# Signs of the last convolution worked out in an early stage, and a partial sum kept on chip

## The chip, the cores and the metric

The kernel runs on one core of one Trainium2 chip. The metric is the device time of one execution in microseconds (us), lower is better. Two versions are compared by a ratio: the mean time of one kernel's fast runs over the mean of the other's fast runs in the same rounds, on the same chip. It is therefore not quite the ratio of the medians that are also quoted. A program counts as faster or slower from 2%. Every kernel was also run once under the profiler, and all times inside an execution are from those single profiles.

## The reference

Two layers on an input of 2 images, 256 channels, 128 x 128 points. Layer 0 is a group norm, three deformable depthwise branches (dilations 1, 9, 12), their sum with a 1x1 convolution, a layer norm, an MLP and a second layer norm. Layer 1 is a group norm and a 3x3 convolution whose weights are reduced to three values.

```python
def _branch(x, w_off, w_def, lw, lb, pad, dil):
    off = _conv(x, w_off, pad, dil)                  # 18 offsets per point
    y = _deform_dw(x, off, w_def, pad, dil)          # bilinear samples, 9 taps per channel
    return gelu(_ln2d(y, lw, lb))
x1, x2, x3 = (_branch(...) for dilation in (1, 9, 12))
out = _ln2d(x1 + x2 + x3 + conv1x1(x), n1_w, n1_b)
out = _ln2d(mlp(out) + out, n2_w, n2_b)              # layer 0: x = x + out of gn(x)
# layer 1
tern = where(w/max > 0.05, 1, where(w/max < -0.05, -1, 0))    # the signs
wq = where(tern > 0, Wp * tern, where(tern < 0, Wn * tern, tern))
x = x + conv3x3(gn(x), wq) + bias
```

## The kernel before

The program has three stages. The *offset stage* computes group-norm statistics of an image, then walks over it in 32 groups of four rows ("columns" below): it normalises, convolves on TensorE, and stores tables of samples and weights ("hats") in memory. Image 1 follows image 0. The *sampling stage* multiplies hats and table rows on TensorE, ScalarE empties PSUM into `ev`, and VectorE adds into three rings of rows, one per branch. A *tail* with its own small scheduler takes finished rows out of the rings through norms and MLP, step by step between the samples; after the last sample it runs alone, which I call the *drain*. The *last stage* is the 3x3 convolution with signs.

The statistics loop of the offset stage uses one tag with three buffers, `xt`:

```python
for b in range(NB):
    for c in range(KC):
        for g0 in range(0, NGRP, XT):
            xt = ap.tile([P, XT * NG], F32, name="xt", tag="xt", bufs=3)   # 1 MB
            nc.sync.dma_start(xt, x[b, ...])
            for j in range(XT):
                nc.vector.bn_stats(stats[:, c, g0 + j, :], xt[:, j * NG : (j + 1) * NG])
    mean, rstd = group_norm(stats, f"gn1_{b}", gps)
    ...
    phase_a(b, ap, psum, k)          # the 32 columns of this image
```

The program's text is put into the engines' order by a scheduler, so an instruction may run well before the place where it is written. The tail of one group of rows of one branch, cut:

```python
if br == 0:
    nc.sync.dma_start(gv, v); return           # written out
other = self.tile("other")
nc.sync.dma_start(other, gv)                   # read again
if br == 1:
    v = v + other                              # VectorE
    nc.sync.dma_start(gv, v); return           # the sum of two is written out
...                                            # br == 2: S = v + 1x1 convolution
pin(nc.vector.tensor_tensor(S, S, other, ALU.add))
```

The rings hold 12, 28 and 32 rows, the tail has 9 buffers of 512 KB (`RINGS = (12, 28, 32)`, `VBUFS = 9`). An addition of two rows is split in two where a ring wraps. The last stage first calls `quantise`: it loads the 2.36 MB of weights, finds their largest absolute value, works out exact thresholds, and makes signs (two comparisons and a difference for each of 18 slices) and sums of signs, all on VectorE, before the convolution can begin.

Of the kernel before, what the change touches and what calls it, by code (L numbers as in the profile page):

```python
# [9 lines left out]
F32 = mybir.dt.float32  # L10
I32 = mybir.dt.int32
U32 = mybir.dt.uint32
BF16 = mybir.dt.bfloat16
# [6 lines left out]
P = 128  # L20
W = 128
# [28 lines left out]
RINGS = (12, 28, 32)  # L50
BRS = (0, 1, 2)
NORMS = 3
VBUFS = 9
# [14 lines left out]
def conv_preact_kernel(ctx: ExitStack, tc: tile.TileContext, t: dict, out: bass.AP):  # L68
# [19 lines left out]

    def load(name, shape, src):
        tl = const.tile(shape, F32, name=name)  # L90
        nc.sync.dma_start(tl, src)
        return tl

    gmask = load("gmask", [P, P], t["gmask"])
    convs = [
# [18 lines left out]

    def dram(name, shape):
        return [scratch.tile(shape, F32, name=f"{name}{b}", tag=f"{name}{b}") for b in range(NB)]
# [8 lines left out]
    yd = scratch.tile([3, C, HW], F32, name="yd")  # L125

# [33 lines left out]
    def phase_a(b, pool, psum, k):  # L160
# [160 lines left out]
        for g in range(NGRP):  # L321
            columns(g)
            while G < H // ZG and min(H - 1, G * ZG + ZG - 1 + max(DILS)) < (g + 1) * R:
                parts = offsets(G)
                for j in range(ZG // R):
                    make_hats(G * (ZG // R) + j, parts, j * R)
                G += 1

    with ExitStack() as actx:
# [18 lines left out]
        nc.sync.dma_start(k["wz"], t["wz"].rearrange("(k p) n -> p k n", p=P))  # L348
        nc.sync.dma_start(k["shift"], t["shift"])
        hatw = ap.tile([P, 2, NTAP * NH], F32, name="hatw32")  # L350
        nc.sync.dma_start(hatw, t["hatw"])
        nc.vector.tensor_copy(k["hatw"], hatw)
        pattern = ap.tile([P, NG], F32, name="pattern")
        nc.sync.dma_start(pattern[HALF : HALF + NPAT], t["pattern"])
        for pl in k["planes"]:
            nc.vector.tensor_copy(
                pl[HALF : HALF + NPAT, 1, :], pattern[HALF : HALF + NPAT]
            )
        for parts in k["parts"]:
            nc.vector.memset(parts, 0.0)  # L360
        XT = min(4, NGRP)
        for b in range(NB):
            stats = ap.tile([P, KC, NGRP, 6], F32, name=f"stats1_{b}", tag=f"stats1_{b}")
            for c in range(KC):
                for g0 in range(0, NGRP, XT):
# [7 lines left out]
                    for j in range(XT):  # L373
                        nc.vector.bn_stats(stats[:, c, g0 + j, :], xt[:, j * NG : (j + 1) * NG])
            mean, rstd = group_norm(stats, f"gn1_{b}", gps)
# [7 lines left out]
            phase_a(b, ap, psum, k)  # L383
# [8 lines left out]
    beyond = nc.values_load(flag[0:1, 0:1], min_val=0, max_val=1)  # L392

# [4 lines left out]
    class Tail:  # L398
# [4 lines left out]
        def __init__(self, pool, psum, pin):  # L403
            self.pool, self.psum, self.pin = pool, psum, pin
            self.waiting, self.running = deque(), []
            self.now = self.last = self.norms = 0
            self.read = set()
# [4 lines left out]
        def may(self, item):  # L412

            others = sum(r[2] for r in self.running if r is not item)
            if self.running and item is not self.running[0]:
                young = others - self.running[0][2] + item[3]
                return young <= VBUFS - PEAK and others + item[3] <= VBUFS
            return others + item[3] <= VBUFS

# [85 lines left out]
        def branch(self, b, br, g, y):  # L505
# [18 lines left out]
            yield 1, 1 + br  # L524
            other = self.tile("other")
            nc.sync.dma_start(other, gv)
            if br == 1:
                yield 2
                pin(nc.vector.tensor_tensor(v, v, other, ALU.add))
                yield 2  # L530
                nc.sync.dma_start(gv, v)
                return
# [12 lines left out]
        def finish(self, b, g, S, other, xn):  # L545
# [3 lines left out]
            for m in range(KC):  # L549
# [8 lines left out]
                )  # L558
            pin(nc.vector.tensor_tensor(S, S, other, ALU.add))
# [65 lines left out]
    def sample_near(pool, psum, k):  # L625

        pin = tc.keep_in_program_order
        tail = Tail(pool, psum, pin)
# [294 lines left out]
    def quantise(pool, signs=None):  # L923

        wq = pool.tile([P, KC, 9, C], F32, name="wq", tag="wq", bufs=1)
        nc.sync.dma_start(wq, t["l1w"].rearrange("(k p) t o -> p k t o", p=P))
        scale = []
        for name in ("wp", "wn"):
            s = pool.tile([P, 1], F32, name=name, tag=name, bufs=1)
            nc.sync.dma_start(s, t[name].partition_broadcast(P))  # L930
            scale.append(s)
        wp, wn = scale
        nc.vector.tensor_scalar(wn, wn, -1.0, None, ALU.mult)

        def col(name):
            return pool.tile([P, 1], F32, name=name, tag=name, bufs=1)

        own, m, mh, ml, pr, er, z, nc_ = (
            col(f"q_{i}") for i in ("own", "m", "mh", "ml", "pr", "er", "z", "nc")
        )  # L940
        nc.vector.tensor_reduce(
            own, wq.rearrange("p k t o -> p (k t o)"), AX.X, ALU.max, apply_absolute_value=True
        )
        nc.gpsimd.partition_all_reduce(m, own, P, bass.bass_isa.ReduceOp.max)  # L944



        def ts(dst, a, s1, op0, s2=None, op1=None):
            nc.vector.tensor_scalar(dst, a, s1, s2, op0, *(() if op1 is None else (op1,)))

        ts(mh, m, 4097.0, ALU.mult)
        nc.vector.tensor_tensor(ml, mh, m, ALU.subtract)
        nc.vector.tensor_tensor(mh, mh, ml, ALU.subtract)
        nc.vector.tensor_tensor(ml, m, mh, ALU.subtract)
        ts(pr, m, THR, ALU.mult)
        nc.vector.scalar_tensor_tensor(er, mh, THR_HI, pr, ALU.mult, ALU.subtract)
        nc.vector.scalar_tensor_tensor(er, mh, THR_LO, er, ALU.mult, ALU.add)
        nc.vector.scalar_tensor_tensor(er, ml, THR_HI, er, ALU.mult, ALU.add)
        nc.vector.scalar_tensor_tensor(er, ml, THR_LO, er, ALU.mult, ALU.add)
        nc.vector.scalar_tensor_tensor(er, m, THR_HALF_ULP, er, ALU.mult, ALU.add)  # L960

        ts(z, m, 0.0, ALU.is_equal)
        nc.vector.tensor_tensor(pr, pr, z, ALU.add)
        ts(nc_, er, -1.0, ALU.mult)
        for k in range(KC):
            for tap in range(9):
                w = wq[:, k, tap, :]
                up = pool.tile([P, C], F32, name="up", tag="up", bufs=1)
                ts(up, w, pr, ALU.subtract, er, ALU.is_ge)
                dn = pool.tile([P, C], F32, name="dn", tag="dn", bufs=1)  # L970
                ts(dn, w, pr, ALU.add, nc_, ALU.is_le)
                if signs is not None:
                    nc.vector.tensor_tensor(signs[:, k, tap, :], up, dn, ALU.subtract)  # L973
                    continue
                ts(up, up, wp, ALU.mult)
                nc.vector.scalar_tensor_tensor(w, dn, wn, up, ALU.mult, ALU.add)
        return wq

# [51 lines left out]
    def phase_c_signs(b, pool, psum, cring, signs, sums, wp, half):  # L1030
# [9 lines left out]
        JC = RC // 2  # L1040
        for g in range(H // RC):
# [4 lines left out]
            for k in range(KC):  # L1046
                nc.sync.dma_start(xl[:, k, rows, :], xv[:, k, lo:hi, :])
            xc = cring[g % len(cring)]
            for k in range(KC):
# [16 lines left out]
                left = D.rearrange("p i j w -> p (i j) w")  # L1066
                for i in range(2):
                    part = xc[:, i, k, :, 1 : 1 + W]
                    nc.scalar.copy(part, left)  # L1069
                    nc.vector.tensor_tensor(  # L1070
                        left if i == 0 else xc[:, 2, k, :, 1 : 1 + W], left, part, ALU.subtract
                    )
            for m in range(KC):
                pc = psum.tile([P, 4, 512], F32, name="pc", tag="pc", bufs=2)

                for bank, t in ((0, 0), (1, 3), (2, 1), (3, 2)):
# [3 lines left out]
                    for j, (k, kx, i) in enumerate(todo):  # L1080
                        w = (
                            signs[:, k, (t // 3 * 2) * 3 + kx] if t % 3 == 0
                            else sums[:, k, t - 1, kx]
# [30 lines left out]

    wpn = small.tile([P, 2], F32, name="wpn", tag="wpn", bufs=1)
    for i, name in enumerate(("wp", "wn")):
        nc.sync.dma_start(wpn[:, i : i + 1], t[name].partition_broadcast(P))
    eq = const.tile([P, 1], I32, name="eq")
    nc.vector.tensor_tensor(eq, wpn[:, 0:1], wpn[:, 1:2], ALU.is_equal)
    same = nc.values_load(eq[0:1, 0:1], min_val=0, max_val=1)  # L1120

    with tc.If(same > 0) as cmp:  # L1122
        with ExitStack() as cctx:
# [10 lines left out]
            signs = cp.tile([P, KC, 9, C], BF16, name="signs")  # L1134
            quantise(cp, signs)

            sums = cp.tile([P, KC, 2, 3, C], BF16, name="sums")
            for k in range(KC):
                nc.vector.tensor_tensor(
                    sums[:, k, 0], signs[:, k, 0:3], signs[:, k, 6:9], ALU.add  # L1140
                )
                nc.vector.tensor_tensor(
                    sums[:, k, 1], sums[:, k, 0], signs[:, k, 3:6], ALU.subtract
                )
                nc.vector.tensor_tensor(
                    sums[:, k, 0], sums[:, k, 0], signs[:, k, 3:6], ALU.add
                )
# [109 lines left out]
```

## Time and profile before

| | before |
|---|---|
| median of the given runs | 7754.24 us (7741.94 to 7755.99) |
| span in the profile | 7751.0 us |
| start of the first sampling matmul | 960.3 us |
| first to last sampling matmul | 5556.9 us |
| drain (to the end of the tail's last addition on VectorE) | 139.4 us |
| from there to the 95th matmul of the last convolution | 84.5 us |
| the rest | 1009.9 us |

The five pieces add up to the span. They are read from the start and end of named instructions in the trace. The page's first part, each engine's busy time with its share of the span and its instructions, and two of its costliest groups (line, engine, operation, tiles, count | busy us, mean ns | idle time before, and what ended it):

```profile
PE 7065.1 (91%) x37984; PEld 5377.1 (69%) x37984; DVE 6136.4 (79%) x12892; ACT 4818.2 (62%) x10138; POOL 708.7 (9%) x1292
...
L762 PE MATMUL pm<-A,xs 128*128 128x180 f32 (+2 forms) x22288 | 3609.6, 318 | 466.8 <-ACT ev L771 438.3
...
L740 DVE SCALAR_TENSOR_TENSOR ring<-ev,defw,ring 128x256 f32<-128x256 f32 (+3 forms) x6272 | 2774.5, 462 | 359.7 <-ACT ev L771 175.2
```

TensorE (PE) is the fullest engine over the whole, and the sampling matmuls wait almost only for ScalarE's eviction (438.3 of 466.8 us of idle time). The last row is the ring addition that shorter rings split more often. The transfers that the change removes are these (same page, list of DMA issues: KB each, us from issue to landing):

```profile
g12d<-T SPq DMA_DIRECT2D x128, 512.0 KB, 7.5
other<-g12d SPq DMA_DIRECT2D x128, 512.0 KB, 10.3
```

Half of each, 64 writes and 64 reads, belong to the sum of two branches.

### The profile page before, as it was taken

How to read it: one execution, taken by the hardware profiler on the slowest of the kernel's cores; microseconds unless marked ns; L12 is line 12 of the kernel's file. 1: busy time of each engine (PE TensorE's matmuls, PEld its weight loads, DVE VectorE, ACT ScalarE, POOL GpSimd, SP SyncE). 2: the span in 40 equal slices, each digit the busy share in tenths (PEclk: the TensorE clock that was granted, in tenths of full speed). 3: DMA queues.
4: the chain of work that ended last, by engine and by line, in shares of the span. 5: the costliest groups of instructions: out<-in, count | busy, mean ns of one | idle time of the engine just before them, and what ended most of it. 6: DMA issues, size and time to landing. Idle time of an engine off the chain costs nothing. (4 is left out here: it accounts for less than half of the span.)

```text
span 7751.0 us, 115301 instructions
## 1 busy us (share of the span) xinstructions
PE 7065.1 (91%) x37984; PEld 5377.1 (69%) x37984; DVE 6136.4 (79%) x12892; ACT 4818.2 (62%) x10138; POOL 708.7 (9%) x1292
## 2 busy tenths in 40 slices
PE   5999888999999999999988999999999998699999
PEld 3555587787877788777777778777887776244444
DVE  6666568888888888888678888888888885677676
ACT  1344366777777777777766777777777776333232
POOL 0000000111111111111101111111111111000000
PEclk9999889999999999999999999999999998799999
DMA  8776799999999999998699999999999994212121
GB/s 296 212 197 190 191 235 249 249 255 251 246 252 252 252 247 251 254 245 229 184 235 247 255 249 250 247 251 255 247 249 253 251 241 133 85 74 75 70 75 49
DMA packets 1011325, 1652.64 MB, mean 213 GB/s; under 512 B 120800, under 2 KB 573200, under 8 KB 1006360
## 3 DMA queue, kind: packets, MB, share of 16 engines
q1 hardware_dynamic: 993304, 1611.57, 77.7%
q10 hardware_dynamic: 17408, 33.56, 1.4%
q8 instruction: 304, 4.98, 0.3%
q14 instruction: 309, 2.53, 0.1%
HBM read 1376.69 MB, written 268.09 MB: 212 GB/s over the span
## 5 line engine op out<-in xcount | busy, mean ns | idle before, releaser
L762 PE MATMUL pm<-A,xs 128*128 128x180 f32 (+2 forms) x22288 | 3609.6, 318 | 466.8 <-ACT ev L771 438.3
L762 PEld LDWEIGHTS pm<-A,xs 128*128 128x128 f32 x22288 | 3407.1, 195 | 680.7 <-ACT ev L771 545.8
L740 DVE SCALAR_TENSOR_TENSOR ring<-ev,defw,ring 128x256 f32<-128x256 f32 (+3 forms) x6272 | 2774.5, 462 | 359.7 <-ACT ev L771 175.2
L771 ACT COPY ev<-pm 128x360 f32<-128x360 f32 (+2 forms) x5572 | 2235.8, 455 | 1131.6 <-DVE ring L740 462.9
L689 DVE TENSOR_TENSOR A<-hy,hx 128x768 f32<-128x768 f32 x1130 | 1022.3, 946 | 424.2 <-DMA hx<-hats 246.5
L487 ACT ACTIVATE T<-T,rs 128x256 f32<-128x256 f32 x1280 | 662.5, 593 | 3.3 <-POOL rs L483 3.2
L480 POOL TENSOR_SCALAR rs<-mv 128x4 f32<-128x4 f32 x320 | 120.7, 377 | 4981.0 <-DVE mv L478 2392.1
L1085 PE MATMUL pc<-cring,signs 128*128 128x512 bf16 x2304 | 521.9, 385 | 57.8 <-DVE signs L973 24.3
L1085 PE MATMUL pc<-cring,sums 128*128 128x512 bf16 x2304 | 510.3, 380 | 0.0
L446 PE MATMUL hp<-T,w 128*128 128x512 f32 x1024 | 492.7, 606 | 12.9 <-ACT T L565 12.9
L476 DVE BATCH_NORM_STATS2 st<-T 128x6 f32<-128x256 f32 x1280 | 446.8, 411 | 23.6 <-ACT T L468 23.6
L1085 PEld LDWEIGHTS <-signs 128*128 128x128 bf16 x2304 | 227.3, 99 | 341.8 <-issue 46.6
L203 PE MATMUL pz<-wz,xa 128*128 128x486 f32 x1024 | 456.7, 579 | 4.3 <-DVE zr L210 4.3
L446 PE MATMUL h<-hT,w 128*128 128x512 f32 x1024 | 460.1, 592 | 0.0
L1085 PEld LDWEIGHTS <-sums 128*128 128x128 bf16 x2304 | 225.4, 98 | 274.4
L515 ACT ACTIVATE T<-zc,bb,bw 128x512 f32<-128x512 f32 x384 | 278.7, 781 | 220.2 <-PE zc L499 219.7
L733 ACT ACTIVATE ring<-ev,defw 128x256 f32<-128x256 f32 (+1 forms) x788 | 392.2, 503 | 24.1
L499 PEld LDWEIGHTS zc<-ident,T 128*128 128x128 f32 x2560 | 325.9, 151 | 97.5 <-issue 61.5
L1093 ACT ACTIVATE o<-xl,l1b 128x1024 f32<-128x1024 f32 x64 | 73.5, 1149 | 505.7 <-DMA out_x<-o 408.3
L499 PE MATMUL zc<-ident,T 128*128 128x128 f32 x2560 | 368.7, 289 | 20.1 <-ACT T L487 13.9
L1069 ACT CAST cring<-D 128x2048 bf16<-128x2048 f32 x128 | 243.3, 1902 | 225.0 <-PE pc L1085 153.7
L482 POOL TENSOR_TENSOR rs<-rs,mhalf 128x4 f32<-128x4 f32 x320 | 368.3, 1151 | 0.0
(120 smaller groups left out, 5814.0 us busy)
## 6 DMA issues: line engine op xcount, KB each, us to landing
hy<-hats SPq DMA_DIRECT2D x1114, 384.0 KB, 6.5
hx<-hats SPq DMA_DIRECT2D x1114, 384.0 KB, 7.4
xs<-table SPq DMA_DIRECT2D x1876, 128.0 KB, 4.4
g12d<-T SPq DMA_DIRECT2D x128, 512.0 KB, 7.5
other<-g12d SPq DMA_DIRECT2D x128, 512.0 KB, 10.3
hats<-hb SPq DMA_DIRECT2D x192, 240.0 KB, 4.3
hats<-hb SPq DMA_DIRECT2D x192, 192.0 KB, 3.4
xl<-x1d SPq DMA_DIRECT2D x56, 640.0 KB, 3.9
```

What stands on the lines that cost most here:

```text
L203: nc.tensor.matmul(pz[:, 0:NZ], lhsT=xt[:, c, r, :], rhs=k["wz"][:, c, :], start=c == 0, stop=c == KC - 1,)
L446: nc.tensor.matmul(out, lhsT=w, rhs=v, start=i == 0, stop=i == n - 1)
L476: pin(nc.vector.bn_stats(st[:, j, :], Tv[:, j, :]))
L482: nc.gpsimd.tensor_tensor(rs[:, 0, :], rs[:, 0, :], mhalf[:, 0:NB4], ALU.pow)
L487: nc.scalar.activation(Tv[:, j, :], Tv[:, j, :], AF.Identity, scale=rs[:, 0, j : j + 1], bias=rs[:, 1, j : j + 1],)
L499: nc.tensor.transpose(zc[:, j * P : (j + 1) * P], Tv[:, j, c * P : (c + 1) * P], ident)
L689: nc.vector.tensor_tensor(dst, hy[:, i0:i1].rearrange("p i t w -> p t i w"), hx[:, i0:i1].rearrange("p i t w -> p t i w"), ALU.mult,)
L733: pin(nc.scalar.mul(dst, src, w))
L740: pin(nc.vector.scalar_tensor_tensor(dst, src, w, dst, ALU.mult, ALU.add))
L762: nc.tensor.matmul(pm[:, j, 0:n], lhsT=xts[b, Rt][T + j][:, c * P : (c + 1) * P], rhs=A[:, m0:m1, AO + (T + j) * CI : AO + (T + j + 1) * C ...
L771: nc.scalar.copy(ev[:, m0:m1, T * CI : (T + 2) * CI].rearrange("p m (t j) -> p t m j", j=CI), pm[:, :, 0:n].rearrange("p t (m j) -> p t m ...
L1085: nc.tensor.matmul(pc[:, bank, :], lhsT=w[:, m * P : (m + 1) * P], rhs=xc[:, i, k, t * JC : (t + 1) * JC, kx : kx + W], start=j == 0, stop ...
```

## The change

It has four intents: take the work for the signs out of the gap before the last convolution and put it where VectorE has room; load constants behind the first image's statistics instead of ahead of them; keep the sum of the first two branches in a buffer till the third branch adds to it; and pay for two more tail buffers with four rows less in two of the rings. The core of the diff, cut:

```diff
-RINGS = (12, 28, 32)
+RINGS = (8, 24, 32)
-VBUFS = 9
+VBUFS = 11
 ...                          # constants: load() only collects, load_now() issues
+    def store_signs(pool):   # a generator, one step per yield
+        def chunk(k, i):
+            w = pool.tile([P, 5, C], F32, name="wk", tag="xt", bufs=3)...
+            nc.sync.dma_start(w, t["l1w"]...[:, k, taps])
+        ...                  # 4 chunks: maxima; thresholds
+        for k in range(KC):
+            sg = pool.tile([P, 15, C], BF16, name="sg", tag="xt", bufs=3)
+            ...              # 2 chunks each: signs and sums of signs
+            nc.sync.dma_start(signd[:, k], sg)
+            yield
 ...
         for g in range(NGRP):
             columns(g)
+            next(beside, None)           # a step of store_signs beside each column
 ...
+        beside = store_signs(ap)
         for b in range(NB):
             ...                          # statistics, xt ring
+            if b == 0:
+                load_now()               # constants, hats' weights, patterns
             ...
-            phase_a(b, ap, psum, k)
+            phase_a(b, ap, psum, k, beside)
 ...
+            kept = self.keep and br == 2
+            yield 1, 2 if kept else 1 + br
+            if kept:
+                while (b, g) not in self.kept:
+                    yield 1
+                other = None
             ...
             if br == 1:
                 pin(nc.vector.tensor_tensor(v, v, other, ALU.add))
+                if self.keep:
+                    self.kept[b, g] = v
+                    return
 ...                          # last stage: one load of ready signs behind the first
+            if first:        # two activation loads; the first tile's split in quarters
+                nc.sync.dma_start(signs, signd)
+                for i in ORDER:
+                    for k in range(KC):
+                        split(xc, k, Ds[k], i, i + 1)
-            quantise(cp, signs)
```

The chunks and the signs take turns in the three `xt` buffers with the statistics' tiles.

## The prediction

> **What bounds the kernel now.** I first read the timeline of the page (its slices), to find the stages, then a table of stretches cut at the stage borders, then the chain of waits, then the instructions in order of time at each border. The kernel has three stages: offsets and tables (0 to 938 us, one start per image), sampling with a tail of normalisations and MLP (944 to 6657), and the last convolution (6660 to 7745). The stretches (TensorE, its weight loads, VectorE, ScalarE, GpSimd, granted clock, DMA share, GB/s):
>
> ```profile
> 0.00:80.00 80.00, 2.52 (x11) 2.23 (x12) 48.35 (x87) 1.28 (x1) 1.40 (x7) 1.00 0.84 305
> 80.00:944.00 864.00, 833.09 (x3391) 464.42 (x3389) 567.89 (x1259) 345.32 (x640) 2.03 (x2) 0.98 0.74 209
> 1100.00:3780.00 2680.00, 2464.70 (x14286) 2119.70 (x14287) 2279.69 (x5118) 1978.87 (x4432) 340.31 (x616) 0.98 0.94 246
> 6500.00:6660.00 160.00, 133.73 (x478) 78.09 (x476) 62.59 (x166) 84.91 (x162) 25.11 (x56) 0.83 0.20 66
> 6660.00:6740.00 80.00, 29.37 (x94) 11.05 (x95) 70.72 (x140) 18.66 (x11) 1.07 (x2) 0.62 0.25 94
> ```
>
> Offsets: TensorE 96% busy, VectorE 66%, DMA 74%: TensorE binds, VectorE and DMA have room. Sampling: TensorE 92%, VectorE 85%, DMA 94% at once; TensorE is the floor and idles 8%. The border at 6660: TensorE works 29 of 80 us while VectorE is full. Why TensorE idles in sampling, from the chain of waits between 1100 and 6500 (total us, times, longest):
>
> ```profile
> PE pm L762 <- ACT ev L771: 418.1, 266, 7.9
> ACT ev L771 <- DVE ring L740: 440.4, 242, 8.7
> DVE A L689 <- DMA hx<-hats: 202.4, 140, 7.3
> DVE A L689 <- DMA other<-g12d: 23.1, 9, 2.6
> ```
>
> TensorE waits for ScalarE to empty PSUM, ScalarE for VectorE to finish with the evicted tile, and VectorE, some of the time, for a transfer. I followed this through a period of six units (two row tiles, three branches, about 86 us, 64 periods in all), with the instructions of the trace between the middle rows of both images: TensorE idles 5.9 us of a period, 2.7 in the first unit and 2.2 in the fifth. In the first VectorE is full (18.9 of 18.8 us, overlaps counted) plus 1.5 us waiting for hats; in the fifth it is full with 0.3 us of such waits. In the second unit VectorE waits 1.0 us for DMA, but TensorE has no gap there.
>
> The border to the last stage, in order of time:
>
> ```profile
> 6659.76 0.38 SPq L926 DMA_DIRECT2D wq<-in_l1w  x1
> 6668.26 4.95 DVE L941 TENSOR_REDUCE q_own<-wq 128x1 f32<-128x4608 f32 x1 [1.81 <-DMA wq<-in_l1w]
> 6673.19 0.87 DVE L154 TENSOR_SCALAR xn<-xl,gn2s_mean,gn2s_rstd 128x1152 f32<-128x1152 f32 x1
> 6713.16 10.48 PE L1085 MATMUL pc<-cring,signs 128*128 128x512 bf16 x36 [18.18 <-DVE signs L973]
> 6729.72 6.09 PE L1085 MATMUL pc<-cring,signs 128*128 128x512 bf16 x15 [6.08 <-DVE signs L973]
> 6735.65 7.97 PE L1085 MATMUL pc<-cring,sums 128*128 128x512 bf16 x36
> ```
>
> The signs are worked out on VectorE between the convolution's own preparation, and TensorE waits 18.2 and 6.1 us for them.
>
> [...] the share alone is no ceiling: 0.84 with 305 GB/s at the start, 0.94 with 246 in sampling. [...] in the groups kept apart by shape:
>
> ```profile
> L740 DVE SCALAR_TENSOR_TENSOR ring<-ev,defw,ring 128x256 f32<-128x256 f32 x2832 | 1355.2, 480 | 248.7 <-ACT ev L771 174.2 <-DVE ring L740 0.9
> L740 DVE SCALAR_TENSOR_TENSOR ring<-ev,defw,ring 128x128 f32<-128x128 f32 x360 | 104.5, 345 | 6.1 <-ACT ring L733 3.0 <-ACT ev L771 1.0
> ```
>
> Half the elements cost 345 ns against 480. [...] Here the clock is 0.62 at the border and 15 matmuls took 6.09 us (0.41 each), where 36 later took 7.97 (0.22).
>
> **The change part by part.**
>
> *Signs moved to the offset stage.* Removed from the border: a 2.3 MB load ahead of the activations, the 4.95 us maximum, 18 times (0.404 + 0.405 + 0.416) = 22 us of thresholds, and 3.3 us of sums. In their place one 1.97 MB load of ready signs behind the first two activation tiles. The first activation now lands near 6664 in the old clock (issued at 6660, 4.0 us to landing as xl does), so the group norm (rstd at 6667.2 before) comes last; then two normalisations and eight differences, 2 x (0.87 + 4 x 0.68) = 7.2 us, of which one half is needed before the first cast. The first tile's split is cut in quarters, so TensorE can begin when signs and a quarter are there: signs need (2 x 0.59 + 1.97) MB at 300 GB/s, 10.5 us[...], about 6673. I let it run unevenly to 6680, when perhaps 14 matmuls are done. Before, 94 were done at 6740. The 80 others at 0.222 us[...] are done at 6700. Gain 40 us. All later work of the stage is TensorE bound and unchanged, with its 18 us gap between the images.
>
> In the offset stage VectorE gets these 22 us and some 10 of maxima, 4% of 864 us at 66% busy, and 6.6 MB of traffic at a share of 0.74: hidden. In the built program the last statistics of image 1 now come after 25 of 32 column groups instead of 15, still before they are needed.
>
> *Loads moved behind the statistics of image 0.* Statistics start waiting on the first 1 MB tile at 24 us and end at 73.3. Some 3 MB of constants no longer stand ahead, at 305 GB/s about 9 us. But the 42 zero writes to the table still take about 29 us of the queue after them (63.9 to 93.5 before), and the third column needs the first table store out: I expect to lose about 4 of the 9 again. Gain 5 us.
>
> *Sum kept on chip.* Removed are 64 writes and 64 reads of 512 KB, 67.1 MB of 1652.64. At 250 GB/s that is 268 us of DMA time, but what counts is where they lie. From the trace, the write is issued in the fourth unit (9.3 us in), the read in the second with three other 512 KB loads (5.2 us in). The big VectorE waits are in the first unit, for hats asked for at the end of the sixth; between, in the early sixth unit, the DMA share falls to 0.2 to 0.5, so the backlog of the second and fourth is gone by then. Only the 0.3 us of the fifth unit is behind a removed transfer: 64 x 0.3 = 19 us.
>
> *Shorter rings.* The order of instructions on TensorE and ScalarE in sampling is almost that of before, and counting while the program is built shows no unit that has to push the tail to free a ring, before or after. But a two-row addition is split where a ring wraps: 64 instructions of 128x256 become 128 of 128x128, and 8 of 244 become 16 of 122: 128 x 0.345 + 16 x 0.338 - 64 x 0.480 - 8 x 0.473 = 15 us more of VectorE, nearly all in the fourth unit, where it is full. So sampling nets 19 - 15 = 4 us; I take 5.
>
> *The drain.* With two more buffers and no third one for the sum, the tail after the last sample needs 53 steps of its scheduler instead of 70 (counted in the built programs). The work is the same: TensorE is busy 134 of 160 us there[...], and before, the last chain ran alone for 16 steps. I give it about half of the 26 idle us: 12 us.
>
> Sum: 40 + 5 + 5 + 12 = 62 us.
>
> **Rivals.** (1) DMA is the bound in sampling: then 67.1 MB less gives up to 268 us, 7486. For it: share 0.94, VectorE waits for hats 202 us. Against: TensorE's 92% leaves about 430 us at most, its waits end at a full VectorE, and the removed transfers are not near the waits. If half of the DMA waits went, about 110 us more: 7580. (2) VectorE takes it back: the splits land where VectorE is full, and the pending sums take buffers (one or two of 11), so chains wait for room. Then sampling loses 10 to 30 us: 7705 to 7730. (3) The border does not shrink fully: after the signs, the wait for x1d, group norm and the splits replaces it, gaining 20 rather than 40: 7710. (4) The later statistics of image 1 delay its start: some 10 us back.
>
> **Range and chances.** 7754.24 - 62 = 7692. The border is sure in sign, sampling uncertain in both directions, and the tail of (1) reaches further down than (2) up. I say 7640 to 7726. Faster by 2% means below 7599: only (1), 0.05. Slower by 2% means above 7909: nothing here adds 155 us, 0.01.
>
> **What would show it.** Right: TensorE's first dense run of the last convolution 17 to 25 us after the last store of the stage before, no waits for signs; sampling between the same unit borders within 20 us of before, its DMA share down by some 4 points with TensorE's idle time little changed; waits for hats still near 200 us; the tail after the last sample 10 to 15 us shorter; statistics done near 64 us. Wrong: if VectorE's waits for hats fall by half and ScalarE's waits for VectorE with them, the DMA was the bound; if the VectorE wait in the fourth and fifth units grows, the splits cost more than they free; if TensorE waits at the start of image 1, the shared buffers of the offset stage did it.

Passages that no trace of this case shows are cut from the prediction and marked. Two terms of the estimate for the border: 2 us for the landing of the signs, with which it came to about 6673 (6660 + 10.5 + 2), and 2 us for slower matmuls at the start, with which it came from 6680 + 80 x 0.222 = 6697.8 to about 6700. The 40 us of the border (6740 - 6700), and with them the sum of 62 us, were worked out with both terms; without the second the border would be about 42 and the sum 64. The 300 GB/s are an estimate from the 305 of the first stretch. "Some 10 of maxima" was an estimate as well; the traces show 4.95 us before and 5.4 us after (four reductions of 1.21 to 1.49 us).

## The result, and the profile after

The changed kernel took 7706.31 us (median of 4 runs, 7692.55 to 7715.61), the kernel before beside it 7751.48 us (4 runs, 7741.94 to 7755.99); the ratio is 0.9942 with a 95% interval of 0.9923 to 0.9961. A second pair on another chip gave 0.9931 (0.9912 to 0.995). The prediction was 7692 in a range of 7640 to 7726.

The five pieces in both pairs of profiles:

| us | before | after | gain | before, 2nd chip | after, 2nd chip | gain | predicted |
|---|---|---|---|---|---|---|---|
| to the first sampling matmul | 960.3 | 977.7 | -17.4 | 972.7 | 977.6 | -4.9 | 5 |
| sampling | 5556.9 | 5549.6 | 7.3 | 5564.7 | 5539.7 | 25.0 | 5 |
| drain | 139.4 | 128.7 | 10.7 | 137.1 | 127.3 | 9.8 | 12 |
| border | 84.5 | 41.6 | 42.9 | 82.9 | 41.7 | 41.2 | 40 |
| rest | 1009.9 | 1011.2 | -1.3 | 1011.2 | 1011.0 | 0.2 | 0 |
| sum | 7751.0 | 7708.8 | 42.2 | 7768.6 | 7697.3 | 71.3 | 62 |

The gains at border and drain repeat within 2 us. The timed gain was 45.2 us in the first (7751.48 - 7706.31) and 58.5 in the second (7767.25 - 7708.76); the profiles of the second pair are a slower than usual run of before and a faster than usual one of after, hence their 71.3. The first two pieces differ between chips by more than the terms that were predicted for them, so they need the experiments.

The page's first part, after:

```profile
PE 7060.7 (92%) x37984; PEld 5373.6 (70%) x37984; DVE 6142.8 (80%) x12979; ACT 4818.2 (63%) x10150; POOL 714.4 (9%) x1292
```

Hardly anything changed in the amount of work: what changed is where TensorE stands idle. The stretches of the kernel after, cut like those of before (stretch and its length; TensorE, weight loads, VectorE, ScalarE and GpSimd busy with instruction counts; granted clock; DMA share; GB/s), the last two shifted to this kernel's drain and border:

```profile
0.00:80.00 80.00, 11.93 (x43) 7.68 (x44) 52.13 (x96) 4.19 (x6) 1.41 (x7) 1.00 0.80 294
80.00:944.00 864.00, 822.55 (x3328) 457.02 (x3327) 584.30 (x1314) 335.69 (x623) 2.40 (x3) 0.98 0.76 214
1100.00:3780.00 2680.00, 2465.20 (x14298) 2119.19 (x14297) 2285.89 (x5150) 1984.25 (x4444) 339.29 (x608) 0.98 0.91 234
6520.00:6650.00 130.00, 116.25 (x412) 67.77 (x412) 53.10 (x152) 76.33 (x141) 25.92 (x56) 0.87 0.14 45
6650.00:6730.00 80.00, 60.28 (x256) 27.02 (x257) 74.63 (x112) 33.10 (x36) 0.69 (x1) 0.81 0.37 141
```

In the first 80 us TensorE now does 43 instructions instead of 11, so it starts earlier; but in 80 to 944 it is busy for 822.55 us where it was 833.09, and does 63 instructions fewer. That stage lost what its start had won. In sampling, DMA moves 234 GB/s instead of 246, and TensorE's busy time is the same to 0.5 us. In the 80 us of the border TensorE does 256 instructions instead of 94.

The chain of waits between 1100 and 6500 (total us, times, longest us):

```profile
ACT ev L909 <- DVE ring L878: 444.9, 250, 7.2
PE pm L900 <- ACT ev L909: 412.0, 270, 6.3
...
DVE A L827 <- DMA hx<-hats: 192.4, 136, 6.4
```

The same three waits stand with nearly the same sums (418.1, 440.4 and 202.4 before); only the 23.1 us for `other` are gone. On the second chip VectorE waited 231.0 us for hats before and 204.9 after. The prediction named a fall of these waits by half as the sign of a DMA bound, and there is none.

The ring additions of both row counts, after:

```profile
L878 DVE SCALAR_TENSOR_TENSOR ring<-ev,defw,ring 128x256 f32<-128x256 f32 x2768 | 1324.9, 481 | 237.7 <-ACT ev L909 167.1
...
L878 DVE SCALAR_TENSOR_TENSOR ring<-ev,defw,ring 128x128 f32<-128x128 f32 x488 | 140.2, 346 | 11.5 <-ACT ring L871 8.7
```

64 double rows less, 128 single rows more, exactly as counted in advance. The idle time before them did not grow in sum: 248.7 + 6.1 us before, 237.7 + 11.5 after. Half the elements cost 346 ns against 481, as before (345 against 480); by the line through the two shapes an estimated 210 ns of an addition do not depend on its length.

The border after, in order of time:

```profile
6660.55 0.36 SPq L1144 DMA_DIRECT2D signs<-signd  x1
...
6670.03 0.58 PE L1183 MATMUL pc<-cring,signs 128*128 128x512 bf16 x1 [4.17 <-DMA signs<-signd]
...
6673.13 0.59 PE L1183 MATMUL pc<-cring,signs 128*128 128x512 bf16 x1 [2.51 <-ACT cring L1130]
...
6674.80 15.38 PE L1183 MATMUL pc<-cring,signs 128*128 128x512 bf16 x57 [1.08 <-DVE cring L1131]
```

The waits of 18.18 and 6.08 us for signs from VectorE are gone. One wait of 4.17 us for the load of the ready signs is left, then short ones for the split of the first tile, and from 6674.80 TensorE runs without a gap, 18.8 us after the end of the tail's last addition at 6655.97; the stage's last store is issued at 6656.00. The prediction named 17 to 25 us after that store as the sign of this step. Up to 6680.3 these matmuls start every 0.43 us, and from 6680.7 on every 0.217; the granted clock was 0.50 from 6670 to 6680 and 0.98 from 6680 to 6700.

### The profile page after: what moved, and what is told of

Its sections match the earlier page's. It is cut to its first block, busy times and chain, and to the rows that moved or that the text cites. A ratio compares the mean times of both kernels' runs of the same rounds, so it can differ in the third digit from the quotient of the medians.

```text
span 7708.8 us, 114916 instructions
## 1 busy us (share of the span) xinstructions
PE 7060.7 (92%) x37984; PEld 5373.6 (70%) x37984; DVE 6142.8 (80%) x12979; ACT 4818.2 (63%) x10150; POOL 714.4 (9%) x1292
## 5 line engine op out<-in xcount | busy, mean ns | idle before, releaser
L878 DVE SCALAR_TENSOR_TENSOR ring<-ev,defw,ring 128x256 f32<-128x256 f32 (+3 forms) x6344 | 2780.3, 459 | 358.5 <-ACT ev L909 167.1
L1183 PE MATMUL pc<-cring,signs 128*128 128x512 bf16 x4608 | 1006.1, 381 | 20.0 <-ACT cring L1130 13.3
L1183 PEld LDWEIGHTS <-signs 128*128 128x128 bf16 x4608 | 452.0, 98 | 573.4 <-issue 28.3
L1130 ACT CAST cring<-D 128x2048 bf16<-128x2048 f32 (+1 forms) x140 | 245.0, 1755 | 184.7 <-PE pc L1183 126.8
L595 ACT COPY T<-tp 128x512 f32<-128x512 f32 x640 | 341.9, 589 | 23.8 <-PE tp L593 23.2
L427 ACT ACTIVATE hb<-ph 96x512 f32<-96x512 f32 (+1 forms) x384 | 211.3, 592 | 187.8 <-PE ph L419 181.8
```

What stands on the lines that cost most here:

```text
L878: pin(nc.vector.scalar_tensor_tensor(dst, src, w, dst, ALU.mult, ALU.add))
L1183: nc.tensor.matmul(pc[:, bank, :], lhsT=w[:, m * P : (m + 1) * P], rhs=xc[:, i, k, t * JC : (t + 1) * JC, kx : kx + W], start=j == 0, stop ...
```

## The experiments

Three calls on three chips; each call has its own runs of the kernel before. Offsets and sizes are read from the profiles, ratios from the timed rounds.

### Signs after the statistics (x1), and again (x1_again)

```diff
-            next(beside, None)
+            if b == 1:
+                next(beside, None)
```

> The changed kernel, with the steps of the signs handed out beside the columns of image 1 instead of image 0; nothing else differs. Measure: when TensorE begins its first sampling matmul (before 960.3 us, changed 977.7), and the time. Theory ORDER (the sign chunks take turns in the three buffers that image 1's statistics also use, so these come later and meet the offset columns for longer): the statistics come early again, first sampling matmul near 955 us, time about 7685 us against 7706 for the changed kernel. Rival TRAFFIC (the 6.6 MB of sign loads and stores cost it, wherever they lie) and rival VECTOR (the 30 us of VectorE work cost it[...]): they move along, first sampling matmul 972 to 980, time 7700 to 7708.

Measured: 7698.36 us (4 runs), ratio 0.9911 (0.9884 to 0.9938). The first sampling matmul started at 960.4 us. Beside the changed kernel on one chip:

> The changed kernel with the signs beside image 1, timed in the same rounds as the changed kernel. ORDER: sampling begins 15 to 25 us before it does in the changed kernel, and the time is 15 to 25 us below that of the changed kernel (0.991 of before against 0.994). If the first result was the chip: equal.

Measured: 7695.52 us (6 runs), ratio 0.9915 (0.9897 to 0.9933); the first sampling matmul at 971.9, 5.7 us before that of the changed kernel (r_after), where ORDER had expected 15 to 25. Of these 5.7 us, 4.9 are there at the group norm of image 0 already (57.7 against 62.6 us), and up to there both kernels issue the same loads and statistics.

The trace shows that this edit does something other than its text says: the scheduler moved the signs' work ahead, from image 1 to 320 to 432 us, beside columns 19 to 26 of image 0. So it swaps the order. In the changed kernel the signs come first (105 to 207 us) and image 1's statistics after them (197 to 376); in x1_again the statistics come first (100 to 249 us).

### The same program pair on one chip (r_before, r_after)

> The kernel before again, for a profile on the same chip as the next three, because the offset stage of two runs of one program differed: with the offset stage of before, TensorE began sampling at 960.3 us on one chip and at 983.4 on another. Expected here: 955 to 990 us, sampling 5550 to 5560 long, drain 139 to 141.

> The changed kernel again, same reason. ORDER says: statistics of image 0 done 10 to 20 us before those of the kernel before on this chip, and all or more of that lost again between the columns 15 and 25, so that sampling begins within 5 us of before or up to 20 later. If the lead is kept to the end (sampling begins 10 to 25 us earlier), the loss in the first pair of profiles was chance, and ORDER falls. Time 0.994 of before.

Measured: before 7770.51 us (1 run; eleven other runs of before have a median of 7767.25), after 7708.76 (6 runs, 7683.79 to 7719.14), ratio 0.9931. Their five pieces are in the table above.

### The kept sum and the rings alone (x3)

The kernel before with the new tail, the short rings and the 11 buffers; signs and constants as before.

> The kernel before with only the sum kept on chip, the shorter rings and eleven buffers; signs and loads as before. If the parts are independent: first sampling matmul at 960 as before, sampling from its first to its last matmul 7 us shorter (5556.9 us before, 5549.6 changed), the drain 11 us shorter (140 to 129), the border as before: 7733 us, 18 us below before. If DMA was the bound of sampling: 7640 or less. If the splits of the shorter rings cost more than the transfers: sampling as long as before or longer.

Measured: 7755.7 us (4 runs), ratio 0.9978 (0.9952 to 1.0004). Drain 128.7 us, border 83.0, sampling 5553.0, first sampling matmul 983.4. The whole gain of the drain is here, none of the border's.

### Signs without their loads (x7), and without their thresholds (x8)

Both are made from the changed kernel. Their outputs are wrong, which doesn't matter for the times. x7 fills the chunks with constants on GpSimd instead of loading them; x8 loads them but does no comparisons and fills the signs on GpSimd.

```diff
-            nc.sync.dma_start(w, t["l1w"]...[:, k, taps])          # x7
+            nc.gpsimd.memset(w, 0.01 * (k + 1) * (2 * i - 1))
-                    up, dn = above(pool, w[:, j, :], limits, sg[:, tap, :])   # x8
-                    nc.vector.tensor_tensor(up, up, dn, ALU.subtract)
+                    nc.vector.tensor_copy(sg[:, tap, 0:1], w[:, j, 0:1])
```

> The changed kernel, whose sign chunks are set by GpSimd instead of loaded (wrong result on purpose: the convolution's signs are meaningless); VectorE's work on them, the buffers and the store stay. TRAFFIC: first sampling matmul back near 955 to 960 us. ORDER or VECTOR: it stays at 970 to 978, though with chunks that are there at once the statistics come some three columns earlier in the program, so ORDER allows 965 to 975.

> The changed kernel, whose sign chunks are loaded but not worked on: one element of each is read, the signs are set to zero by GpSimd (wrong result on purpose); loads, buffers and store stay. VECTOR: first sampling matmul back near 955 to 960 us. TRAFFIC: stays at 970 to 978. ORDER: the statistics stand three columns earlier in the program than in the changed kernel, so 965 to 975.

Measured: 7702.79 and 7702.92 us, one run each; first sampling matmul at 978.6 and 980.0. Neither moves it from the changed kernel's 977.6. Both ran on another chip, where x1 began sampling at 960.4. Neither the chunks' traffic alone nor the thresholds' VectorE work alone is what is lost. ORDER had expected 965 to 975, since the statistics of image 1 come earlier here: they did (133.6 to 329 us in x7, 164 to 337 in x8, against 197 to 376), and nothing came back. The replacement costs GpSimd little (its fills took 9.8 us in x7 and 6.6 us in x8), but it is not nothing.

### Long rings with the kept sum (x5)

x1 with rings of 12, 28 and 32 rows and 9 buffers.

> The changed kernel with the signs beside image 1, the sum kept on chip, but the rings of before (12, 28, 32 rows) and nine buffers as before. Counted while it is built: 69 steps to drain the tail after the last sample (53 in the changed kernel, 70 before), no push by a ring. If the prediction's sum for sampling is right (transfers near the fifth unit 19 us, splits 15 us), sampling is about 15 us shorter than with the short rings (5529 against 5544) and the drain 10 to 12 us longer (139 against 127): within 5 us of that kernel in all. If the splits cost nothing: sampling as with the short rings, 12 us slower in all.

Measured: 7685.56 us (4 runs), ratio 0.9903 (0.9882 to 0.9924). Sampling 5537.8 us against 5539.5 in x1_again on the same chip, drain 135.1 against 127.3. The splits of the short rings cost sampling nothing that shows; but x3 and x7, which sample alike, lie 12.3 us apart on one chip (5553.0 and 5540.7), so one pair of profiles is weak against an expected 15. Two more buffers, together with the shorter rings, are worth 7.8 us in the drain.

### The sum written out again (x6)

x1 without keeping: the 67.1 MB are back, rings and buffers stay short and 11.

```diff
-        tail = Tail(pool, psum, pin, True)
+        tail = Tail(pool, psum, pin)
```

> The version with the signs beside image 1 (x1), with the sum of the first two branches written out and read again as in the kernel before; short rings and 11 buffers stay, and the drain keeps its 53 steps of the tail's scheduler (counted in the built program). If the removed transfers are what shortened the sampling (the prediction's term of 19 us): first to last sampling matmul about 5557 us against 5540 in x1, DMA in the sampling back at about 250 GB/s from 239, the wait of VectorE for a transfer in the fifth unit back at 0.3 to 0.6 us a period from 0.2, and the whole about 0.2% longer than x1's 0.991. If they are hidden anyway and the gain comes from elsewhere: sampling within 5 us of 5540 with the traffic back. Drain in both cases about 127 us, if the buffers and not the kept sum shortened it; about 140 if the kept sum did.

Measured: 7697.16 us (4 runs), ratio 0.9926 (0.9904 to 0.9948); sampling 5551.1 us; drain 127.3. The stretch from 1100 to 6500, first x1_again, then x6 (columns as above), with the wait that came back:

```profile
1100.00:6500.00 5400.00, 4971.61 (x28788) 4268.14 (x28788) 4601.29 (x10360) 3994.91 (x8927) 683.27 (x1220) 0.98 0.91 234
```

```profile
1100.00:6500.00 5400.00, 4965.51 (x28726) 4257.35 (x28727) 4592.16 (x10345) 3980.02 (x8908) 679.75 (x1220) 0.98 0.93 245
```

```profile
DVE A L828 <- DMA other<-g12d: 25.6, 10, 2.6
```

Bandwidth and the old wait are back as expected, 11 GB/s and 25.6 us. Sampling is 7 us longer than the mean of the ten profiles with kept sum and short rings (after 5549.6, r_after 5539.7, x1 5543.9, x1_again 5539.5, x3 5553.0, x7 5540.7, x8 5541.3, x9 5543.2, x10 5543.1, x12 5550.9; mean 5544.5). But the largest of the ten is 5553.0, and x12, which keeps the sum, took 5550.9 on the same chip as x6, so 7 us lie inside their spread. It is a third of the predicted 19 us, or nothing. The six-unit period, averaged over the middle rows, points to nothing: 86.18 and 86.44 us in the two profiles of before, 86.03 and 85.99 in those of after, and 86.04 in x6, with the transfers back. What shortened sampling between before and after is then not found. The drain stayed at 127.3, so the kept sum did not shorten it: that leaves the buffers and the shorter rings, which no run separates.

### Late statistics alone (x12)

x1 with the three `xt` buffers held by constant tiles up to column 11 of image 0, so that image 1's statistics are late as in the changed kernel but no signs stand before them.

```diff
+        def hold(columns):
+            tiles = [ap.tile([P, XT * NG], F32, name="ht", tag="xt", bufs=3) for _ in range(3)]
+            for h in tiles:
+                nc.gpsimd.memset(h, 1.0)
+            ...                    # `columns` steps, then each tile is read once
-            if b == 1:
-                next(beside, None)
+            next(beside if b == 1 else held, None)
```

> Tests the order of the statistics alone. x1 with the three shared buffers of the offset stage held by three constant tiles till about column 11 of image 0, so that the statistics of image 1 stand beside columns 14 to 24 (14 to 25 in the changed kernel, 7 to 17 in x1), with no chunks of the signs' weights and no thresholds there. If the late statistics alone lose the lead (order): the first sampling matmul starts about 975 to 980 us, column 25 near 418, against about 966 and 400 in the other runs of this call with x1's offset stage; the whole about 10 us longer than x1. If it is the chunks together with the late statistics: within 4 us of those runs.

Measured: the statistics ran from 183 to 335 us, as late as meant; the first sampling matmul started at 959.5 us, against 959.8 and 965.3 in x6 and x9. By the profile, late statistics alone delay nothing at the end of the stage. The timed runs do not agree so clearly: 7708.42 us (4 runs), ratio 0.994 (0.9918 to 0.9962), 11 us above x6, as the theory of order had expected, though x6 even has the removed transfers back; the intervals overlap, and the profiled run was the fastest of the four (7694.93). I take the theory of order alone as not supported, and not as ruled out.

### The first tile's split whole (x9)

```diff
-            first = b == 0 and g == 0
-            if first:
+            first = False
+            if b == 0 and g == 0:
                 nc.sync.dma_start(signs, signd)
```

> x1 with the first tile of the last convolution split whole and not in quarters. If the quarters matter for the border, as the prediction took it: the end of the tail to the 95th matmul of the last convolution takes 45 to 50 us instead of 40. If TensorE waits for the signs anyway and the whole split is done by then: still 40 us.

Measured: 7694.13 us (1 run), border 45.1 us against 39.9 in x1_again and 39.7 in x6. TensorE at the border, x9 first, then x1_again:

```profile
6652.04 1.01 PE L1184 MATMUL pc<-cring,signs 128*128 128x512 bf16 x2 [6.47 <-ACT cring L1131]
6656.36 1.01 PE L1184 MATMUL pc<-cring,signs 128*128 128x512 bf16 x2 [3.31 <-ACT cring L1131]
```

```profile
6652.69 0.58 PE L1184 MATMUL pc<-cring,signs 128*128 128x512 bf16 x1 [4.18 <-DMA signs<-signd]
6655.78 0.58 PE L1184 MATMUL pc<-cring,signs 128*128 128x512 bf16 x1 [2.50 <-ACT cring L1131]
```

With the whole split TensorE no longer waits for the signs' load at all: the cast comes later than it. With quarters the load of the signs is the later one. Both ends are close together, so the quarters are worth 5 us of the 42.

### Constants ahead again (x10)

x1 with the constants loaded before the statistics of image 0.

> x1 with the constants loaded before the statistics of image 0, as in the kernel before. The prediction gave the moved loads 9 us at the group norm and kept 5 of them. So: the group norm's matmul at 65 to 75 us instead of 55 to 58, and the first sampling matmul 5 us later than in the other runs of this call with x1's offset stage; if the zero writes and the stores of the table take the lead back, less than 3 us later; if all survives, 10 or more. Earlier runs of one program lay up to 10 us apart on different chips, so only the same call is compared.

Measured: 7718.74 us (1 run). The group norm's first matmul came at 77.7 us, against 57.5 and 55.4 in x6 and x9, and the first sampling matmul at 991.0 against 959.8 and 965.3. The stretch from 60 to 80 us, x10 first, then x9:

```profile
60.00:80.00 20.00, 1.18 (x4) 1.01 (x4) 14.88 (x29) 0.00 (x0) 0.00 (x0) 1.00 0.81 286
```

```profile
60.00:80.00 20.00, 19.77 (x63) 10.70 (x62) 9.79 (x20) 4.50 (x8) 0.00 (x0) 1.00 0.65 200
```

TensorE is at full work in one and has not begun in the other. Against these two runs the moved loads give some 20 us at the group norm, and nothing of it is lost on the way to the sampling. The size varies: up to the group norm all runs with moved loads do the same, and it came at 54.9 to 64.9 us in them, against 67.5 to 79.1 in before, r_before, x3 and x10; in the two pairs of before and after the lead was only 9.5 and 4.9 us. One thing differs from before: in x10 the hats' weights and patterns also pass through the three `xt` buffers ahead of the statistics.

### Where the offset stage loses it

The trace gives the start of each column of image 0 (its first offset matmul). In us:

| profile | signs' place | group norm | columns 8 to 25 | 25 to 32 | first sampling matmul |
|---|---|---|---|---|---|
| before | last stage | 74.4 | 234.6 | 115.4 | 960.3 |
| r_before | last stage | 67.5 | 238.8 | 117.7 | 972.7 |
| x3 | last stage | 79.1 | 236.6 | 118.5 | 983.4 |
| after | before statistics | 64.9 | 264.0 | 115.4 | 977.7 |
| r_after | before statistics | 62.6 | 261.9 | 115.4 | 977.6 |
| x7 (no loads) | before statistics | 56.8 | 260.3 | 117.7 | 978.6 |
| x8 (no thresholds) | before statistics | 56.6 | 263.4 | 117.6 | 980.0 |
| x1 | after statistics | 55.2 | 243.8 | 127.6 | 960.4 |
| x1_again | after statistics | 57.7 | 252.9 | 121.8 | 971.9 |
| x5 | after statistics | 55.3 | 248.0 | 126.3 | 964.9 |
| x6 | after statistics | 57.5 | 243.3 | 124.1 | 959.8 |
| x9 | after statistics | 55.4 | 245.3 | 125.2 | 965.3 |
| x12 (held) | after statistics | 54.9 | 250.0 | 118.9 | 959.5 |
| x10 (constants ahead) | after statistics | 77.7 | 246.1 | 115.4 | 991.0 |

Columns 8 to 25 separate the groups: 235 to 239 us without signs, 243 to 253 with the signs after the statistics, 260 to 264 with the signs before them. But such a cut misleads on its own: the signs of the middle group fall in columns 19 to 26 and lengthen those after 25, and image 1's statistics, which start at column 2 where the constants are loaded ahead, start at column 4 or later where they are not. From the group norm to the start of column 32, all of image 0, it is 443 to 461 us without signs (before, r_before, x3), 458 to 472 with the signs after the statistics and 472 to 479 with the signs before them. On the one chip that ran all three, it is 460.9 (r_before), 472.0 and 466.1 (x1_again, x5) and 471.6 (r_after). So the loss goes with the signs in either order; what the order adds is not shown, since profiles of one and the same offset stage lie up to 14 us apart here (458.3 in x6, 472.0 in x1_again).

How the time is lost can be read too. Over the same stretch TensorE idles 23.5, 32.4 and 32.0 us without signs, 40.7 and 41.1 in the two profiles of after, and 35 to 42 with the signs after the statistics. From 60 to 980 us its wait for `parts`, an operand that VectorE prepares, grew most, and VectorE's wait for rows of the image (`xa`) grew with it; before first, then after:

```profile
DVE xa L154 <- DMA xa<-in_x: 43.0, 31, 6.8
...
PE pp L290 <- DVE parts L280: 10.9, 5, 6.2
```

```profile
DVE xa L173 <- DMA xa<-in_x: 62.1, 36, 4.6
...
PE pp L407 <- DVE parts L397: 26.3, 10, 4.4
```

The stretch from 260 to 420 us of before, after, x1_again and x12, in this order:

```profile
260.00:420.00 160.00, 157.90 (x658) 88.93 (x656) 103.64 (x232) 68.26 (x128) 0.00 (x0) 1.00 0.75 210
```

```profile
260.00:420.00 160.00, 140.35 (x518) 74.63 (x517) 106.50 (x226) 52.81 (x99) 0.00 (x0) 0.89 0.78 227
```

```profile
260.00:420.00 160.00, 145.67 (x565) 78.22 (x563) 112.46 (x271) 56.54 (x105) 0.38 (x1) 0.94 0.78 220
```

```profile
260.00:420.00 160.00, 144.04 (x578) 79.63 (x578) 129.92 (x301) 61.14 (x115) 0.38 (x1) 0.97 0.86 246
```

In before, this stretch has neither statistics nor signs beside it (its statistics ran from 105 to 238 us), and TensorE runs 658 matmuls at full clock. In after it has the statistics of image 1: 518 matmuls, and the granted clock is 0.89. Part of this is only later instead of earlier: from 60 to 420 us it is 1282 matmuls in before, 1202 in after and 1286 in x12. In columns 8 to 25, where the same matmuls stand, both waiting and slower matmuls count: idle time 11.4 us in before and 30.5 in after, busy time 223.2 and 233.5. VectorE is busy only 106.50 of 160 us in after's stretch, so it was not for want of VectorE time in the sum.

## Why the prediction was right or wrong

**The total was right, its make-up partly not.** 7692 predicted, 7706.31 and 7708.76 measured, both inside the range. Border and drain were worked out and came true; that the errors in the other two pieces left the sum in the range was partly luck.

**Border: right.** 40 us predicted, 42.9 and 41.2 measured; x3, which has all but signs and constants, keeps 83.0, and x10, which has the constants back ahead, keeps the gain (41.3), so it is the signs that did it. The "one 1.97 MB load of ready signs behind the first two activation tiles" was the last thing that TensorE waited for before its first matmul, at 6670 instead of the estimated 6673, and that "The first tile's split is cut in quarters" is worth 5 us (x9). Rival (3), a border that gains only 20, falls.

**Drain: right.** 12 predicted, 10.7 and 9.8 measured. By x6 and x5 it comes not from the kept sum but from the two more buffers, as counted in advance (53 steps against 69), or the shorter rings that came with them: 127.3 without keeping and with 11 buffers and short rings, 135.1 with keeping, 9 and long rings.

**"Only the 0.3 us of the fifth unit is behind a removed transfer: 64 x 0.3 = 19 us": mechanism not refuted, size too large.** The wait in the fifth unit fell from 0.30 to 0.16 us a period, and on the second chip from 0.57 to 0.25, but with the transfers back in x6 it was 0.23. The transfers cost at most some 7 us by x6, inside the spread of the profiles.

**"15 us more of VectorE, nearly all in the fourth unit, where it is full": the count was right, its price was not.** The fourth unit lasted 13.04 us before and 13.05 after. The busy time of the line rose by 2780.3 - 2774.5 = 5.8 us and not 15: the 488 single rows at 346 ns are 168.8 us one by one, but the line was busy with them for 140.2, so their records overlap. x5 shows no gain from long rings. Where 15 us were charged, none show on the path. Rival (2), a loss of 10 to 30 us in sampling, falls. Two terms that were both too large in size nearly cancelled, which was luck, and the sampling came out 7.3 and 25.0 us shorter instead of 5. How much of the difference between these two numbers is the chip, one profile each cannot say.

**Rival (1), a DMA bound: falls.** 67.1 MB less took the sampling from 245 to 234 GB/s and its share from 0.94 to 0.91, and putting them back changed the sampling by at most some 7 us of 5544.

**"Hidden": wrong, the step that failed.** The prediction put the signs' work in the offset stage at no cost, since VectorE was 66% busy and DMA at a share of 0.74 over 864 us, and because the statistics came "still before they are needed". Averages over the stage said nothing about the columns where the work falls. What the runs showed in place of no cost: from the group norm to column 32 image 0 took 471.9 and 471.6 us against 443.5 and 460.9 (28 and 11 us more), with TensorE's idle time there up from 23.5 and 32.4 us to 40.7 and 41.1. Columns 8 to 25 took 23 to 29 us longer than in the three profiles without signs; the lead of 9.5 and 4.9 us at the group norm had become a lag of 17.4 and 4.9 at the first sampling matmul. Rival (4) came near in size ("some 10 us back"), not in mechanism: it let late statistics delay the start of image 1, but these end at 376 us, image 1's group norm comes at 513, and TensorE waits there for nothing longer than 0.9 us. The loss lies earlier, in image 0's columns beside which signs and statistics run. Nor are late statistics enough by themselves: x12 has them as late, and by its profile sampling starts at 959.5.

**"I expect to lose about 4 of the 9 again": wrong in the other direction.** The lead at the group norm was 9.5 and 4.9 us in the two pairs, near the 9, and some 20 us in x10's comparison, where all of it reaches the sampling. The two errors in this stage have opposite signs, which is why the loss there is small.

**What stays open.** Within the signs' cost before the statistics, x7 and x8 took away loads and thresholds one at a time and got nothing back. What those two and the changed kernel share, and x1 and x12 lack, is that chunks and signs take turns in the three `xt` buffers, and that the signs are stored, while the first columns run. Whether either lengthens the columns, no run shows. Rival VECTOR and rival TRAFFIC are refuted only one at a time: loads and VectorE work together stay possible. And since the same program began sampling at 960.3 and 972.7 us on two chips, the order's share, which is nothing in the stretch from the group norm to column 32 on the one chip that ran both (471.6 and 472.0), is not settled.

**Is there a better version?** With the signs after the statistics the ratios are 0.9911 and 0.9915, with long rings besides 0.9903, against 0.9931 of the changed kernel in the same rounds as the last two. Their medians are 13 and 23 us lower. The intervals overlap, so x5 is the best median here and not a shown improvement.

## What to carry to other kernels

Room in an engine's average over a stage did not make new work free here: the average was 66%, VectorE was busy 106.50 of 160 us even in the stretch that lost, and TensorE still waited for VectorE. Look at which waits of the full engine end at the engine that gets the work, in the columns where a scheduler will put it. Work taken off the end of a stage, where one engine visibly waits for it, paid as computed (42 us against 40); transfers and splits inside a stage with a full engine showed less than half of what they were computed at here. When two chips differ by 10 us and more at the same point (960, 973 and 983 us here for one offset stage), terms of 5 us need a direct experiment.
